# Weighted context sums of a Perceiver block: classical products against seven Strassen products, one core of a Trainium2 chip

## The chip, the core and the metric

The kernel runs on one core of one Trainium2 chip. The time is device time in microseconds for one launch, the median of three runs. A core has a matrix engine (TensorE, "PE" in the profile, with its weight loads as "PEld"), a vector engine (VectorE, "DVE"), a scalar engine (ScalarE, "ACT"), GpSimd ("POOL") and SyncE ("SP"), which here only issues transfers. Each engine works through its own queue in order; semaphores tie the queues together. All the arithmetic of this kernel is in 32-bit floats.

## The reference

One block of a Perceiver: cross attention from 8 x 64 latents to a context of 8 x 1601 rows, then causal self attention, then a feed-forward part with ternary weights, each with a residual. The change lies in the cross attention, whose core is:

```python
q = (hidden_states @ Wq).reshape(B, Sq, H, D)          # B=8, Sq=64, H=16, D=128
k = (encoder_hidden_states @ Wk).reshape(B, Skv, H, D) # Skv=1601, context width 256
v = (encoder_hidden_states @ Wv).reshape(B, Skv, H, D)
q = rmsnorm(q, gq)
k = rmsnorm(k, gk)
scores = jnp.einsum('bqhd,bkhd->bhqk', q, k) * scale
attn = jax.nn.softmax(scores, axis=-1)
out = jnp.einsum('bhqk,bkhd->bqhd', attn, v)
return out.reshape(B, Sq, H * D) @ Wo
```

The kernel never forms the values of all 1601 rows. It sums the context rows themselves with the softmax's probabilities (a 256 x 512 result for a batch and half of the heads) and multiplies by Wv afterwards. These sums are the "weighted context sums".

## The kernel before, in words

**Units and steps.** The work of cross attention is cut into 16 units `u`: a batch entry `b` and a half `g` of the heads (8 heads of 64 queries, 512 columns). A unit has 1601 context rows: 12 full blocks of 128 and a tail of 65, numbered `j` = 0 to 12. Two full blocks make a pair, and `step(u, q)` (L928) handles one pair `q` = 0 to 5. So there are 96 steps, and in the main loop the order on TensorE, VectorE, ScalarE and GpSimd is the order in which the code calls the instructions (`manual_schedule`). SyncE's transfers are placed by the framework around this.

**Keys and scores of a step.** A step needs the norms of the keys of its 256 rows (products of 128x512, called `p_u`, `p_5`, `p_2`) and the raw scores of the rows (products of 128x256, called `s_a`, `s_2`). Both are already made by Strassen's scheme in Winograd's form: seven products in place of eight, with sums of operands made on GpSimd (`cxS`, L212 to L215, from the transposed context `cxT`; `aT`, L247 to L250, from the queries) and sums of results on ScalarE and VectorE. A product in 32-bit floats is two TensorE instructions in the profile. The bank `p_u` carries a chain of growing sums: first product, copied away by ScalarE (`p1`), then a second product on top, copied (`u2`), a third on top, added to `p5` by VectorE (`c22`, L1017), and a fourth on top, whose squares ScalarE sums in place (`squares`, L720). `c12` (L999) and `c11` (L1046) are the other two blocks of keys; all four blocks are squared and summed by ScalarE in 16 pieces. At the start of the next step the squares become factors (`rsqrt_into`), VectorE scales the scores (L690) and keeps a running maximum `mx` (L704, L706).

**Softmax of the unit before.** While unit `u` grows its scores, unit `u-1` gets its probabilities: VectorE subtracts the maximum (`less_max`, L785) and ScalarE takes exponentials in place (L789) in steps 1 to 4, in portions listed in `PROBS`; GpSimd adds them up into `den` (`add_to_sums`, L796, L798), three blocks in step 1, two in step 2, three in step 3 and four in step 4. A tiny copy `gate` (L1005) keeps GpSimd from starting before the running maximum of the step is done. The maximum over rows is found in step 0 (`find_max`), and spread over the partitions by products of ones with two parts of a diagonal, a rounded high part and the rest (`spread_diag`, L735, `spread_max`, L760). The sums `den` are spread and inverted in step 5.

**Weighted sums.** `weigh_context(u, j)` (L800) adds block `j` into two banks `y0`, `y1` of 128x512: for each half of the context's columns one product of 128x512, so four TensorE instructions a block. `weigh(k)` (L918) hands out the next `k` blocks of unit `u-1`, with a lag: one behind the first `p_u`, one ahead of the third product of `p_u` (`product_7`), and in step 1 two behind `product_7` in place of the latter. `finish` (L834) multiplies the two banks by the inverted sums on VectorE, in step 1. After the loop come the last blocks of unit 14, the values of the first heads, and unit 15's softmax and weighted sums, then Wo, self attention and the feed-forward part.

**Banks and buffers.** The eight banks of PSUM: tags `k` (two, for `p_u`), `s` (two, for `s_a`, `s_2` and the tail scores), `m` (two, for `p_5`, `p_2` and spreading) and `y0`, `y1`. The tag `t2` is a set of 12 buffers of 128x512 in SBUF for everything that is kept for a while; `s` has 7 buffers of 128x2x512 for the scores; `cxn` 5 buffers of one block of context.

Of the kernel before, what the change touches and what calls it, by code (L numbers as in the profile page):

```python
# [28 lines left out]
def perceiver_kernel(  # L29
# [127 lines left out]

    xs = ctx.enter_context(ExitStack())
    ctxp = xs.enter_context(tc.tile_pool(name="ctxp", bufs=1, side="right"))

    CXN = 5
    cxn, cxT = {}, {}

    def load_context(u, j):
        b, r = u // G, rows(j)
        t = ctxp.tile([P, C], F32, tag="cxn", name="cxn", bufs=CXN)
        nc.sync.dma_start(t[:r, :], cx[b, j * P : j * P + r, :])
        cxn[u, j] = t

    NB = 4 * NC
# [3 lines left out]
    def load_blocks(b, q):  # L176

        t = ctxp.tile([P, NC, 8, 32], F32, tag="cxB", name="cxB", bufs=2)
        src = cx[b, 2 * q * P : 2 * (q + 1) * P, :].rearrange(
            "(ki kj) (c ci cj) -> ci kj c ki cj", kj=32, c=NC, cj=32  # L180
        )
        for i in range(4):
            nc.sync.dma_start(t[32 * i : 32 * i + 32], src[i])
        cxB[b, q] = t
# [7 lines left out]
    def transpose_context(b, q):  # L192
# [4 lines left out]
        t = ctxp.tile([P, NC, 2 * P], F32, tag="cxT", name="cxT", bufs=6)  # L197
# [8 lines left out]
        if (b, q) == (0, 0):  # L206
            sums = ctxp.tile([P, 4, P], F32, tag="cxB", name="cxS", bufs=2)
        else:
            sums = work.tile([P, 4, P], F32, tag="og", name="cxS", bufs=HG)
        s1, s2, s3, s4 = [sums[:, i, :] for i in range(4)]  # L210
# [451 lines left out]
    def new_ksq():  # L662
        return work.tile([P, 4, HD], F32, tag="t2", name="ksq", bufs=12)

    def tail_scores(u):
        b, g = divmod(u, G)
        sp = ps.tile([P, HG, S], F32, tag="s", name="sp")
# [30 lines left out]
    def keep_max(u, j):  # L698
# [3 lines left out]
        if j == 1:  # L702
            mx[u] = work.tile([P, HG, S], F32, tag="t2", name="mx", bufs=12)
# [4 lines left out]
    def bank(name, tag="m"):  # L708
        return ps.tile([P, 4 * HD], F32, tag=tag, name=name)

    def kept(name):
        return work.tile([P, 4 * HD], F32, tag="t2", name=name, bufs=12)
# [14 lines left out]
    def load_contexts(k):  # L727

        nonlocal n_cx
        while n_cx < min(k, NU * NJ):  # L730
            u, j = divmod(n_cx, NJ)
            load_context(u, j)
            n_cx += 1

    def spread_diag(col):  # L735
# [4 lines left out]
        lo = small.tile([P, W // P], FR, tag="clo", name="clo", bufs=2)  # L740
        nc.vector.tensor_tensor(lo, col, hi.bitcast(F32), ALU.subtract)
        dg = []
        for part in (hi, lo):
            d = work.tile([P, W // P, P], FR, tag="t2", name="dg", bufs=12)
            nc.vector.tensor_tensor(
                d,
                ident.unsqueeze(1).to_broadcast([P, W // P, P]),
                part.bitcast(F32).unsqueeze(2).to_broadcast([P, W // P, P]),
                ALU.mult,
            )  # L750
            dg.append(d.rearrange("p a k -> p (a k)"))
        return dg
# [7 lines left out]
    def spread_max(u):  # L760
        bp = spread(mB[u])
        mB[u] = work.tile([P, HG, S], F32, tag="t2", name="mB", bufs=12)
# [28 lines left out]
    def add_to_sums(u, j, eng):  # L791
        r = rows(j)
        s = s_sb[u, j]
        if j == 1:
            den[u] = work.tile([P, HG, S], F32, tag="t2", name="den", bufs=12)
# [3 lines left out]

    def weigh_context(u, j):  # L800
        b, g = divmod(u, G)
        r = rows(j)
        if j == 0:
            yps[u] = [
                ps.tile([P, HG, S], F32, tag=f"y{c}", name=f"y{c}", bufs=1)
                for c in range(NC)
            ]
        s = s_sb.pop((u, j))
        s_pair.pop((u, j // 2), None)
        for c in range(NC):  # L810
            nc.tensor.matmul(  # L811
                yps[u][c],
                cxn[u, j][:r, ts(c, P)],
                s[:r],
# [3 lines left out]

    def find_sum(u):
        rB[u] = [  # L820
            work.tile([P, W], FR, tag="t2", name=f"den{n_}", bufs=12) for n_ in "hl"
# [3 lines left out]
    def spread_sum(u):  # L825
        bp = spread(rB[u])
        rB[u] = work.tile([P, HG, S], F32, tag="t2", name="rB", bufs=12)
# [6 lines left out]
    def finish(u):  # L834

        b, g = divmod(u, G)
        for c in range(NC):
            nc.vector.tensor_tensor(
                a_sb[g][c][:, :, ts(b, S)], yps[u][c], rB[u], ALU.mult
            )  # L840

    LAG = 3
    NQ = 3 * NF
    tiles = [(b, j) for b in range(B) for j in range(NJ)]
    pairs = [(b, q) for b in range(B) for q in range(NJF // 2)]
    n_tp, n_q, n_cx, n_av = 1, 0, 0, -LAG
# [18 lines left out]
    def piece(name, single, dtype=F32):  # L865
# [772 lines left out]
```

## Time and profile before

| | |
|---|---|
| runs (us) | 1682.91, 1682.92, 1683.78; median 1682.92 |
| span of the profiled execution | 1681.5 us |
| what lies around the span, against the median | 1.4 us |
| PE busy | 1670.3 us, 99% of the span |
| DVE, ACT, POOL busy | 1193.6 (71%), 1155.3 (69%), 449.8 us (27%) |
| granted TensorE clock | 1.00 in all windows of the loop |
| one unit in the loop (start of VectorE's `chi` to the next unit's, 596.29 to 675.90) | 79.61 us |

The page's groups give for each line the summed busy time, the mean length of one instruction, and the idle time just before them with what ended it. TensorE's instructions are pipelined and their ends are modelled: a 128x512 instruction is listed with 592 ns, but the next one starts 430 ns after it. Where the cost of a product is wanted, the distance between starts has to be taken. In this document "step 1" always means `q` = 1 of a unit.

### The profile page before, as it was taken

To read this page: it belongs to the slowest core of one execution; us is meant where nothing else is said; L and a number is where in the kernel's file an instruction comes from. 1 tells how busy PE (TensorE), PEld (TensorE's weight loads), DVE (VectorE), ACT (ScalarE), POOL (GpSimd) and SP (SyncE) were. 2 spreads that over 40 slices of the span, in tenths; PEclk is the share of its full clock that TensorE was granted. 3 is DMA by queue.
4 is the path that set the end of the run, shared out by engine and by line. 5 is a ranking of instruction groups with operands and counts; after the bars stand their busy time and mean duration, and the time that the engine had idled before them with its cause. 6 is when DMAs were issued, how large, how long until landed. Compare 5 with 4: busy or idle time off the path is not lost.

```text
span 1681.5 us, 20165 instructions
## 1 busy us (share of the span) xinstructions
PE 1670.3 (99%) x5484; PEld 955.9 (57%) x5484; DVE 1193.6 (71%) x1922; ACT 1155.3 (69%) x4511; POOL 449.8 (27%) x592
## 2 busy tenths in 40 slices
PE   9999999999999999999999999999999999999999
PEld 5755555555555555555555555555555554466787
DVE  5447878787887878787878787888778786235641
ACT  5668887878787777777787878787877773023441
POOL 3312132423242323232232324232323122000040
PEclk9999999999999999999999999999999999999999
DMA  7002221212222222122222212221221216400330
GB/s 216 1 7 36 38 48 41 59 39 46 44 50 44 43 50 46 44 43 49 48 45 46 48 40 50 49 51 38 46 47 35 68 43 240 137 1 1 101 101 25
DMA packets 255769, 92.61 MB, mean 55 GB/s; under 512 B 209936, under 2 KB 236328, under 8 KB 255656
## 3 DMA queue, kind: packets, MB, share of 16 engines
q1 hardware_dynamic: 246298, 68.78, 18.6%
q0 software_dynamic: 8928, 22.02, 4.4%
q8 instruction: 43, 0.70, 0.2%
q14 instruction: 70, 0.57, 0.1%
q10 hardware_dynamic: 430, 0.53, 0.1%
HBM read 77.62 MB, written 7.34 MB: 51 GB/s over the span
## 4 chain that ended last, share of the span: by engine, by line
PE 96%; ACT 2%; DVE 2%; issue 0%; POOL 0%; POOLq 0%; DVEq 0%; ACTq 0%
PE y L811 21%; PE p_u L716 19%; PE s_a L716 14%; PE p L716 14%; PE gu L1453 4%; PE op L897 3%; PE s L716 2%; PE kp L286 2%; PE fop L1567 2%; PE mm_qk L1248 2%; PE q_u L406 2%; PE aps L502 2%; PE vp L882 2%; PE sp L669 2%; PE q L406 1%; PE bp L110 1%
## 5 line engine op out<-in xcount | busy, mean ns | idle before, releaser
L720 ACT ACTIVATE c<-c 128x128 f32<-128x128 f32 x1152 | 340.6, 297 | 140.6 <-DVE c L1017 57.7
L811 PE MATMUL y<-s,cxn 128*128 128x512 f32 x768 | 356.9, 592 | 0.0
L811 PEld LDWEIGHTS y<-s,cxn 128*128 128x128 f32 x768 | 144.5, 190 | 151.7 <-issue 138.9
L720 ACT ACTIVATION_READ_ACCUMULATOR c<-c 128x1 f32 x1152 | 215.2, 187 | 0.0
L798 POOL TENSOR_TENSOR den<-den,s 128x512 f32<-128x512 f32 x150 | 190.7, 1271 | 43.5 <-ACT s L789 36.4
L716 PEld LDWEIGHTS s_a<-aT,cxS 128*128 128x128 f32 x576 | 109.3, 190 | 137.9 <-issue 126.3
L1005 POOL COPY gate<-mx 128x1 f32<-128x1 f32 x60 | 11.0, 183 | 618.9 <-DVE mx L704 287.5
L716 PE MATMUL s_a<-aT,cxS 128*128 128x256 f32 x576 | 171.3, 379 | 0.0
L690 DVE TENSOR_TENSOR s<-s,ssq 128x1024 f32<-128x1024 f32 x96 | 116.9, 1218 | 24.9 <-ACT ssq L105 24.7
L706 DVE TENSOR_TENSOR mx<-mx,s 128x512 f32<-128x512 f32 x160 | 114.1, 713 | 7.6
L789 ACT ACTIVATE s<-s,zero_t 128x1024 f32<-128x1024 f32 (+1 forms) x117 | 115.9, 991 | 4.6 <-DVE s L785 4.6
L785 DVE TENSOR_TENSOR s<-s,mB 128x1024 f32<-128x1024 f32 (+1 forms) x117 | 116.4, 1017 | 2.2 <-ACT mB L763 2.1
L1017 DVE TENSOR_TENSOR c<-p_u,p 128x512 f32<-128x512 f32 x96 | 64.9, 676 | 71.5 <-PE p_u L716 71.5
L1042 DVE TENSOR_TENSOR s<-s_a,half 128x512 f32<-128x512 f32 x96 | 66.1, 688 | 57.1 <-POOL den L798 41.1
L720 ACT ACTIVATE p_u<-p_u 128x128 f32<-128x128 f32 x384 | 99.9, 260 | 9.3
L716 PE MATMUL p_u<-wkS,cxT 128*128 128x512 f32 x192 | 98.5, 594 | 0.9 <-DVE c L1017 0.9
L716 PE MATMUL p_u<-wkS,cxS 128*128 128x512 f32 x192 | 98.2, 593 | 0.9 <-ACT p L953 0.9
L716 PE MATMUL p<-wk,cxS 128*128 128x512 f32 x192 | 98.2, 593 | 0.0
L716 PE MATMUL p<-wkS,cxS 128*128 128x512 f32 x192 | 98.1, 592 | 0.0
L716 PE MATMUL p_u<-wk,cxS 128*128 128x512 f32 x192 | 98.0, 592 | 0.0
L716 PE MATMUL p<-wk,cxT 128*128 128x512 f32 x192 | 98.0, 592 | 0.0
L716 PE MATMUL p_u<-wk,cxT 128*128 128x512 f32 x192 | 98.0, 592 | 0.0
(239 smaller groups left out, 3254.0 us busy)
## 6 DMA issues: line engine op xcount, KB each, us to landing
cxn<-in_ctx_dram SPq DMA_DIRECT2D x192, 128.0 KB
cxB<-in_ctx_dram SPq DMA_DIRECT2D x192, 64.0 KB
wf<-in_L_ffn_w_gate_up_dram SPq DMA_DIRECT2D x32, 256.0 KB
fgu<-fw POOLq DMA_DIRECT2D x4, 2048.0 KB, 8.4
fw<-wT SPq DMA_DIRECT2D x192, 32.0 KB
wq<-in_L_xattn_Wq_dram SPq DMA_DIRECT2D x4, 1024.0 KB
wf<-in_L_ffn_w_proj_dram SPq DMA_DIRECT2D x16, 256.0 KB
wo<-in_L_xattn_Wo_dram POOLq DMA_DIRECT2D x16, 256.0 KB, 6.8
```

The source lines that it names most:

```text
L406: nc.tensor.matmul(out_, a[:, c], b[:, c], start=first, stop=True, skip_group_check=not first)
L690: nc.vector.tensor_tensor(flat, flat, kr.unsqueeze(2).to_broadcast([P, 2 * HG, S]), ALU.mult)
L706: nc.vector.tensor_tensor(mx[u][:r], mx[u][:r], s[:r], ALU.max)
L716: nc.tensor.matmul(out_, a, w, start=start, stop=True, skip_group_check=not start)
L720: nc.scalar.activation(k[:, ts(h, HD)], k[:, ts(h, HD)], AF.Square, accum_out=ssq[:, 4 * half + h : 4 * half + h + 1],)
L785: nc.vector.tensor_tensor(t, t, m.to_broadcast([r, len(js), W]), ALU.subtract)
L789: nc.scalar.activation(t, t, AF.Exp, bias=zero_t[: t.shape[0]], scale=1.0)
L798: eng.tensor_tensor(den[u][:r], den[u][:r], s[:r], ALU.add)
L811: nc.tensor.matmul(yps[u][c], cxn[u, j][:r, ts(c, P)], s[:r], start=(j == 0), stop=(j == NJ - 1),)
L1017: nc.vector.tensor_tensor(c22, p_u, p5, ALU.add)
L1042: nc.vector.tensor_tensor(quarters[:, 1::2], s_a, half[:, 0:2], ALU.add)
L1453: nc.tensor.matmul(gu[:, cols], fgu_sb[rr // 8][:, rr % 8, c, :], xs_[n_][c][:, cols], start=(c == 0 and n_ == 0), stop=(c == ND - 1 and n ...
```

## The change

The weighted sums of units 0 to 14 are made from seven products a pair of blocks instead of eight half-size ones: the 256x256 piece of context (a pair of row blocks, two halves of columns) and the 256x512 piece of probabilities are cut into 2x2 blocks, and Winograd's seven products of 128x256 go into seven half banks of four banks `y0` to `y3`. As the sums of results are linear, they are made once a unit.

- `context_sums` makes three sums of 128x128 and overwrites one block, four GpSimd operations a pair; `prob_sums` makes three sums of 128x256 (`yT`, one buffer) and overwrites a block of the probabilities, four GpSimd operations a pair.
- `pair_products` yields the seven products: three at the end of a step, two behind the next step's first `p_u`, two ahead of its `product_7`. `tail_products` adds the tail's rows in step 0.
- `gather_first` and `gather` put the seven sums together in step 1 of the unit after next: a copy on ScalarE, one 128x512 and four 128x256 additions on VectorE, two 128x256 additions on GpSimd, and the two 128x512 multiplications by the inverted sums on GpSimd; `finish` on VectorE remains for unit 15.
- Banks: `k` and `s` have one bank each, `y0` to `y3` one each, `m` two; `s_2` and the tail scores move to `m`. The squares of `c11` are moved behind those of `p_u` and the copy of the last score block.
- The maximum is rounded to its high part: `spread_diag` makes one diagonal, and the spreading product has one part.
- Context is loaded a pair at a time, three buffers of 256 rows. `t2` has 10 buffers, the scores 8; `cxS` has three sums and takes the fourth in place; other buffers move to suit. After the loop, tiles that alternated in `k` and `s` alternate with `y2` and `y3`.

The core of the diff:

```diff
-    CXN = 5
+    CXN = 3
...
+    T2 = 10
...
-        s1, s2, s3, s4 = [sums[:, i, :] for i in range(4)]
+        s1, s2, s4 = [sums[:, i, :] for i in range(3)]
+        s3 = a21
...
     def bank(name, tag="m"):
-        return ps.tile([P, 4 * HD], F32, tag=tag, name=name)
+        return ps.tile([P, 4 * HD], F32, tag=tag, name=name, bufs=2 if tag == "m" else 1)
...
-        lo = small.tile([P, W // P], FR, tag="clo", name="clo", bufs=2)
-        nc.vector.tensor_tensor(lo, col, hi.bitcast(F32), ALU.subtract)
-        dg = []
-        for part in (hi, lo):
...
+        return [d.rearrange("p a k -> p (a k)")]
...
+    def context_sums(u, p):
...
+        eng = nc.gpsimd
+        eng.tensor_tensor(s1, a21, a22, ALU.add)
+        eng.tensor_tensor(s2, s1, a11, ALU.subtract)
+        eng.tensor_tensor(s4, a12, s2, ALU.subtract)
+        eng.tensor_tensor(a21, a11, a21, ALU.subtract)
+        yA[u, p] = a11, a12, a22, s1, s2, a21, s4
...
+    def prob_sums(u, p):
+
+        (b11, b12), (b21, b22) = prob_blocks(u, p)
+        t1, t2_, n4 = [yT[:, i, :] for i in range(3)]
+        eng = nc.gpsimd
+        eng.tensor_tensor(t1, b12, b11, ALU.subtract)
+        eng.tensor_tensor(t2_, b22, t1, ALU.subtract)
+        eng.tensor_tensor(b12, b22, b12, ALU.subtract)
+        eng.tensor_tensor(n4, b21, t2_, ALU.subtract)
+
+    def pair_products(u, p):
...
+        for k, h, a, b_, first in (
+            (0, 0, a11, b11, True),
+            (1, 0, a12, b21, True),
+            (2, 0, s4, b22, True),
+            (0, 1, s1, t1, False),
+            (1, 1, s2, t2_, False),
+            (3, 1, s3, t3, True),
+            (2, 1, a22, n4, False),
+        ):
+            product(yps[u][k][:, ts(h, W // 2)], a, b_, first and p == 0)
+            yield
...
+    def gather_first(u):
+
+        y0, y1 = yps[u][:2]
+        c15 = kept("c15")
+        nc.scalar.copy(c15, y0)
+        cu = kept("cu")
+        nc.vector.tensor_tensor(
...
+        cw = kept("cw")
+        nc.gpsimd.tensor_tensor(
+            cw[:, : W // 2], cu[:, W // 2 :], c15[:, W // 2 :], ALU.add
+        )
...
+    def gather(u):
...
+        add = nc.vector.tensor_tensor
+        add(u3, q7, u2, ALU.add)
+        c21 = c15[:, : W // 2]
+        add(c21, q4, u3, ALU.add)
+        add(u3, t22, u3, ALU.add)
+        add(u2, q3, u4, ALU.add)
+        nc.gpsimd.tensor_tensor(c5, u3, c5, ALU.add)
+        b, g = divmod(u, G)
+        for c, t in enumerate((cu, c15)):
+            nc.gpsimd.tensor_tensor(
+                a_sb[g][c][:, :, ts(b, S)],
+                t.rearrange("p (h s) -> p h s", s=S),
+                rB[u],
+                ALU.mult,
+            )
...
+    def pair_of(u, q):
+        v, p = (u - 1, q - 1) if q else (u - 2, NQU - 1)
+        return (v, p) if v >= 0 else None
...
     def step(u, q):
...
-        if u > 0:
-            weigh(1)
-        elif q < n_tails - 1:
+        weigh(2)
+        if q == 1 and u > 1:
+            gather_first(u - 2)
+        if new:
+            context_sums(*new)
+        if u == 0 and q < n_tails - 1:
...
+        weigh(9)
+        if q == 0 and u > 1:
+            tail_products(u - 2)
+        if q == 1 and u > 1:
+            gather(u - 2)
         if probs:

             nc.gpsimd.tensor_copy(gate, mx[u][:, 0, 0:1])
         for js in probs:
             for j in js:
                 add_to_sums(u - 1, j, nc.gpsimd)
...
+        if new:
+            prob_sums(*new)
+        if u > 1 or (u == 1 and q > 1):
+            load_contexts(n_cx + (2 if q == 0 else 1))
...
         product_7()
         squares(ssq[:, 1], 1, c22)
-        if u > 0 and q == 1:
-            weigh(2)
...
-        squares(ssq[:, 0], 0, c11)
         next(roots, None)
         product(p_u, a22, n4, False)
         squares(ssq[:, 1], 0, p_u)
-        s_2 = ps.tile([P, 4, S], F32, tag="s", name="s_2")
+        s_2 = bank("s_2")[:, : 4 * S].rearrange("p (h s) -> p h s", s=S)
...
         nc.scalar.copy(quarters[:, 2], s_a[:, 1])
+        squares(ssq[:, 0], 0, c11)
+        if new:
+            under_way = pair_products(*new)
+            weigh(3)
...
-        for jw in range(NJ - LAG, NJ):
-            load_contexts((last - 1) * NJ + jw + CXN)
-            weigh_context(last - 1, jw)
+        context_sums(last - 1, NQU - 1)
+        weigh(9)
+        prob_sums(last - 1, NQU - 1)
         find_max(last)
+        tail_products(last - 1)
         mB[last] = spread_diag(mB[last])
-        finish(last - 1)
+        under_way = pair_products(last - 1, NQU - 1)
+        weigh(5)
+        gather_first(last - 1)
+        weigh(9)
+        load_contexts(NU * NY)
+        gather(last - 1)
```

## The prediction

> **What bounds the kernel now.** The page comes first: who is busy, what chain ended last, and the costliest groups.
>
> ```profile
> PE 1670.3 (99%) x5484; PEld 955.9 (57%) x5484; DVE 1193.6 (71%) x1922; ACT 1155.3 (69%) x4511; POOL 449.8 (27%) x592
> ...
> PE 96%; ACT 2%; DVE 2%; issue 0%; POOL 0%; POOLq 0%; DVEq 0%; ACTq 0%
> ...
> L811 PE MATMUL y<-s,cxn 128*128 128x512 f32 x768 | 356.9, 592 | 0.0
> ```
>
> TensorE never stops: every microsecond of products that goes is won, and every wait that comes is paid. Second, the waits of TensorE; each kind comes to under 3 us, so the other engines have some cover everywhere, but the view does not say how much.
>
> ```profile
> PE p_u L716 <- ACT p L953: 0.9, 2, 0.7
> PE p_u L716 <- DVE c L1017: 0.9, 2, 0.4
> ```
>
> Third, the timeline of TensorE for the true price of a product (two instructions a line, distance between starts).
>
> ```profile
> 592.35 0.59 PE L716 MATMUL s_a<-a,cxT 128*128 128x256 f32 x2
> 592.78 1.02 PE L716 MATMUL p_u<-wkS,cxS 128*128 128x512 f32 x2
> 593.64 1.02 PE L716 MATMUL p<-wk,cxS 128*128 128x512 f32 x2
> ```
>
> A 128x256 product costs 0.43 us, a 128x512 one 0.86: half the columns, half the time, weight load hidden. Fourth, step 1 of a unit, where the change puts most of its new work: the stretch that begins with its first `p_u`, then the timelines of VectorE, TensorE and GpSimd in it, then two groups of GpSimd by form.
>
> ```profile
> 601.85:616.89 15.04, 15.04 (x44) 7.97 (x43) 11.56 (x19) 11.34 (x47) 5.75 (x8) 1.00 0.21 44
> ```
>
> ```profile
> 605.00 1.28 DVE L838 TENSOR_TENSOR a<-y,rB 128x512 f32<-128x512 f32 x2
> ...
> 610.41 0.65 DVE L1017 TENSOR_TENSOR c<-p_u,p 128x512 f32<-128x512 f32 x1
> ```
>
> ```profile
> 609.15 3.60 PE L811 MATMUL y<-s,cxn 128*128 128x512 f32 x8
> ...
> 614.31 1.02 PE L716 MATMUL p_u<-wkS,cxT 128*128 128x512 f32 x2
> ```
>
> ```profile
> 612.37 2.62 POOL L798 TENSOR_TENSOR den<-den,s 128x512 f32<-128x512 f32 x2 [1.62 <-ACT s L789]
> ```
>
> ```profile
> L247 POOL TENSOR_TENSOR aT<-a 128x256 f32<-128x256 f32 x16 | 14.2, 888 | 65.9 <-issue 34.4 <-PE s_a L716 31.5
> ...
> L249 POOL TENSOR_TENSOR aT<-a,a 128x256 f32<-128x256 f32 x16 | 11.9, 743 | 13.7 <-PE s_a L716 13.7
> ```
>
> VectorE ends `c22` (L1017) only 3.2 us ahead of the `p_u` product that needs it, and the two blocks of `weigh(2)`, 3.44 us, are what stands between. GpSimd is busy 5.8 of 15 us; its sums of 512 columns follow each other every 1.31 us (two in 2.62; the mean of one in the groups is 1.27).
>
> **What is won.** A pair of blocks now takes four products of 512, 3.44 us; after, seven of 256, 3.01 us. The tail costs 1.72 us both ways. Six pairs in 15 units: 90 x 0.43 = 38.7 us. The spreading of the maximum loses its second part, an instruction of 0.22 us, in 16 units: 3.5 us. Together 42.2 us off TensorE, all on the path.
>
> [...] The rows above show 215 and 430 ns here, and they are used.
>
> **What is added on GpSimd.** A pair: four sums of 128x128 at 0.46 (the `cxS` groups' mean) and four of 128x256 at about 0.77 (743 to 888 in the rows), 4.9 us; a unit's `gather`: two of 128x256 at 0.73 (L250's mean) and two multiplications of 512 columns at 1.31 (the nearest row is `den`), 4.1 us. A unit's 24.5 us of GpSimd become about 58 of 80. On the whole it fits; in step 1 it does not. There the code sets GpSimd's order: the small `cw`, `context_sums`, `gather`'s sum and two multiplications, `gate`, three `den` sums, and only then `prob_sums`, whose first two results TensorE wants as its second and third product of step 2. Clock from step 1's first `p_u`:
>
> - TensorE ends the last two products of the old pair at 6.45: four key products 3.44, three of `s_a` 1.29, four of y 1.72.
> - VectorE starts late, since the bookkeeping of step 0's weights (L622 to L633, 2.4 us) now ends at 1.0; then `less_max` 1.14, `cu` behind ScalarE's copy `c15` (2.6 to 3.3), `less_max` to 4.4, scaling to 5.7, maximum to 6.3, `c12` to 6.9. The additions depend on each other, 0.45 us each: the third is done at 8.2.
> - GpSimd: 8.3 + 0.73 + 2 x 1.31 + 0.15 (`gate`) + 3 x 1.31 = 15.7; first result of `prob_sums` 16.5, second 17.25.
> - TensorE, unhindered, starts step 2 at 12.04 (seven products each of 0.86, 0.43 and 0.43) and wants these two at 12.90 and 13.33. The second can start at about 17.35.
>
> So 4.0 us are lost from step 1 to step 2. About 0.8 of that falls in step 1: VectorE does the fourth addition, a transpose and `c22` until 9.8, and the fourth `p_u` product, wanted at 9.03, waits, as `weigh(2)` no longer stands ahead of it. The rest is the wait for `prob_sums`. It is one loss, not two. Bounds: with no gap between instructions (1.27, 0.73) and VectorE never late, 3.3; with all GpSimd work stretched as L247 is against L249 (888 to 743), 5.8. I take 4.0, since the chain is made of rows of the same shapes. Units 2 to 15: 14 x 4.0 = 56 us. Later steps catch up: in step 2 GpSimd has two `den` sums, and its second result comes 1 us ahead of need. In step 4, with four, it is about 0.6 us ahead; if that is gone, 0.5 us a unit.
>
> **One bank for growing keys.** The next step's first `p_u` now waits for the squares of the last.
>
> ```profile
> 1370.22 0.25 ACT L720 ACTIVATE p_u<-p_u 128x128 f32<-128x128 f32 x1
> ...
> 1370.62 0.26 ACT L720 ACTIVATE p_u<-p_u 128x128 f32<-128x128 f32 x1
> ```
>
> Each piece starts 0.40 after the one before, so the four take 1.6 us, and where ScalarE is free they start 0.25 after the product: 1.85. Between stand `s_2`, the last `s_a` and three products of y: 2.15. It fits by 0.3 where ScalarE is on time. In step 4 it is not: there its queue has three exponentials, and the old cover of 1.72 us ahead of `product_7` is 0.86; the squares end some 0.4 too late. I take 0.3, bounds 0 and 0.6, in 15 units: 4.5 us. In unit 0 and step 0 of unit 1 there are no y products: 0.86 of cover for 1.85, seven times 1.0; TensorE's waits in that stretch (2.7 us) are partly taken up: 6 us, bounds 3 and 10.
>
> **After the loop** the values wait for `gather` of unit 14: 1.35 of additions, 0.73 and 2.62 on GpSimd, where `finish` took 1.28: 4 us, bounds 2 and 6.
>
> **Costed at nothing.** VectorE: `finish`, `clo` and a diagonal go (2.1 us a unit), 2.3 come; what matters is counted above. ScalarE: one copy more. SyncE's loads: as many bytes, issued behind the y products that free the buffer, a step and a half ahead of use; if late, `context_sums` waits, which has some 2 us of cover in step 1. Ten `t2` buffers: `p1` and `p5` of step 2 wait for `gather`'s multiplications, done at 10.4 and 11.7, ahead of both. `c11` of step 1 waits for GpSimd's sum at 9.0, earlier than its own product.
>
> **The sum**, against the execution's own time (span 1681.5 plus 1.4, the median 1682.9): 1682.9 - 42.2 + 56 + 4.5 + 6 + 4 = 1711.2; I say 1711.
>
> **Rivals.** *A, the other side: GpSimd keeps up.* If the products of step 2 found `prob_sums` ready, because the wait is short or TensorE has other delays in front that cover it, the sum is 1682.9 - 42.2 + 14.5 = 1655. It decides at a wait of (42.2 - 14.5) / 14 = 2.0 us a unit: below that the change is faster. For it: GpSimd idles 73% of the time, and no TensorE wait on it is seen now. Against: the chain is queue order, and half of it is five operations of a length the profile shows 150 times.
>
> *B: the doubled work on GpSimd and VectorE slows both.* Stretched by a fifth, the chain is 1.8 us longer: 14 x 1.8 = 25 us more, 1736. For: 888 against 743 ns for one shape. Against: `den` keeps 1.27 beside a busy VectorE. [...]
>
> *C: single banks cost a wait in every step.* If ScalarE is late by 0.4 us beyond the margin in half of the 90 steps, 18 us more, 1729; in all, 1747. For: ScalarE is at 62 of 80 us a unit and would have 77. Against: squares of `c11` are moved out of the way.
>
> **How the numbers follow.** Forecast 0.55, A 0.1, B 0.15, C 0.15; the rest, 0.05, is a wait somewhere near 2 us, on either side of the old time. Forecast's own bounds: 3.3 us gives 1701, the others' lower ends 1692; upper ends with 4.6 us 1728. The range runs from 1692 to 1738, which takes in B and half of C and leaves A out. A measurement of this kernel can tell about 0.2%, 3.4 us. Faster 0.11, same 0.02, slower 0.87.
>
> **What would show it.** Right: a TensorE wait on GpSimd's L853 or L854 of about 3 us, 14 times, one on VectorE's `c22` of some 0.8 in step 1, a unit of 81 us, and the span of y instructions cut by 38 us. Wrong: no such wait (A), GpSimd's 512-column sums over 1.4 us (B), or first `p_u` products that wait on ScalarE in most steps (C).

## The result

The changed kernel takes 1890.04 us (median of four runs, 1888.44 to 1893.08) against 1683.08 for the kernel before on the same chip: a ratio of 1.1232, 95% interval 1.1218 to 1.1246. It is 12% slower. The forecast was 1711 with a range up to 1738; the sign was right and the size was not.

The profiled execution has a span of 1888.9 us, 207.4 more than before. First the lines of its page that answer to those shown of before (busy time, the chain that ended last, the costliest group of the weighted sums with the idle time ahead of it):

```profile
PE 1723.1 (91%) x6068; PEld 1079.5 (57%) x6068; DVE 1376.1 (73%) x1935; ACT 1163.4 (62%) x4526; POOL 1165.4 (62%) x1372
...
PE 57%; DVE 18%; POOL 14%; ACT 7%; issue 3%; DMA 0%; POOLq 0%; DVEq 0%; ACTq 0%
...
L732 PE MATMUL y<-yT,yS 128*128 128x256 f32 x360 | 115.2, 435 | 66.5 <-POOL yT L853 48.3
```

TensorE was hardly ever idle before (11.2 us of the span) and is idle for 165.8 us now. The chain, which was 96% TensorE, runs through VectorE and GpSimd for a third of the time. Two things in the first line are odd. VectorE has 13 instructions more and is busy for 182 us more. And TensorE is busy for 53 us more, although 42 us of products were taken away.

The waits of TensorE, longest in total first (us in total, times, longest):

```profile
PE y L732 <- POOL yT L853: 48.3, 21, 5.2
PE bp L110 <- DVE st L694: 27.5, 12, 3.0
PE p_u L732 <- ACT p_u L736: 20.3, 16, 1.7
PE y L732 <- POOL yT L854: 18.1, 24, 1.2
```

The first and the last are the wait for `prob_sums`: of the 21 waits for L853, 14 stand in step 2, where the prediction has them, and 7 of 1.0 to 1.3 us in step 5 of every second unit. The second is in no step of it: the spreading product of step 5 waits for a bank `m` that the tail scores hold until VectorE has read them (L694).

Where it happens is seen in windows of one unit, cut at each step's first `p_u` (columns: window, length, busy time of TensorE, its weight loads, VectorE, ScalarE, GpSimd, then the granted clock). The steps 0 to 5 of this unit last 14.67, 13.27, 18.81, 12.05, 14.59 and 20.46 us; the same unit before had 13.37, 14.18, 12.46, 12.47, 12.46 and 14.67. These are steps 2, 3 and 5:

```profile
681.53:700.34 18.81, 15.56 (x44) 9.40 (x43) 12.80 (x16) 10.46 (x45) 17.81 (x22) 0.82 0.20 39
700.34:712.39 12.05, 12.05 (x44) 7.98 (x43) 11.13 (x16) 9.93 (x43) 8.39 (x10) 1.00 0.21 44
...
726.98:747.44 20.46, 16.68 (x49) 9.27 (x48) 16.43 (x23) 9.70 (x44) 16.30 (x22) 0.92 0.08 11
```

Step 3 has no wait and is the change as it was meant: 12.47 became 12.05, 0.42 less. Steps 2 and 5 lose 6.4 and 5.8 us, and in both the granted clock is below 1. The timeline of TensorE and one more window show the second half of that price:

```profile
685.17 1.22 PE L732 MATMUL y<-yT,yS 128*128 128x256 f32 x2 [2.62 <-POOL yT L853]
687.02 1.22 PE L732 MATMUL y<-yT,yS 128*128 128x256 f32 x2 [0.63 <-POOL yT L854]
688.04 1.91 PE L732 MATMUL p<-wkS,cxS 128*128 128x512 f32 x2
```

```profile
685.17:692.00 6.83, 6.20 (x11) 3.69 (x12) 5.00 (x5) 0.89 (x2) 6.65 (x7) 0.50 0.25 29
```

The `p` product at 688.04 is followed by the next one 1.70 us later, not 0.86. From the end of the 2.62 us wait TensorE runs at half its clock for 6.83 us. Over the whole span the mean granted clock is 0.968; as it is either 1.00 or 0.50 (in all 552 whole windows of the grid below), 6.4% of the span, 121 us, ran at half, and that costs 60 us of full-speed products. This is most of why TensorE is "busy" for longer with less to do: 53 us more, and 42 us of products less, make 95. The other 35 are what a wait costs beyond its idle time. In step 1 the product ahead of the wait for `c22` starts at 676.43, the one behind it at 678.40 and the next at 679.37, which is 1.22 us more than twice 0.86, for a wait listed with 0.95. At 0.27 us each, the some 120 waits that came would make 32 us (an estimate). So the loss adds up: 155 us of idle time, 60 of halved clock and 35 of this, less 42 of products, are 208.

A wait of 2.62 us was enough for this. All the changes of the clock in this trace lie a whole number of 3.413 us apart (the halvings at 685.17 and 736.37, for example, 15 of them). Four windows of this grid follow: one with the wait of 2.62 us, one with most of a wait of 2.97 (for L694, until 736.78), and two that share another wait for L694 of 2.96 (until 922.42):

```profile
681.76:685.17 3.41, 0.79 (x3) 0.01 (x1) 3.34 (x3) 1.91 (x9) 3.27 (x3) 1.00 0.03 4
...
732.96:736.37 3.41, 0.86 (x4) 0.40 (x3) 3.34 (x4) 1.17 (x2) 3.23 (x4) 1.00 0.00 0
...
917.28:920.69 3.41, 2.00 (x7) 1.06 (x6) 3.38 (x4) 1.17 (x2) 3.25 (x5) 1.00 0.00 0
920.69:924.11 3.42, 1.69 (x5) 1.05 (x6) 2.31 (x4) 0.67 (x2) 3.22 (x5) 1.00 0.00 0
```

TensorE is busy for 0.79 and 0.86 us in the first two, and the clock is halved from the end of each, before the 0.63 us wait in the one case and inside the wait in the other. It is busy for 2.00 and 1.69 us in the last two, and the clock stays. In the kernel after, a window at full clock with 1.93 us of idle time or more was always followed by half clock (26 windows), one with 1.67 us or less never, and of nine in between one. So a wait's place on the grid counts as well as its length.

Last, what VectorE and GpSimd do to each other. Both timelines in step 1, VectorE first:

```profile
671.16 1.22 DVE L795 TENSOR_TENSOR s<-s,mB 128x1024 f32<-128x1024 f32 x1
672.29 1.75 DVE L706 TENSOR_TENSOR s<-s,ssq 128x1024 f32<-128x1024 f32 x1
```

```profile
671.32 1.64 POOL L905 TENSOR_TENSOR cw<-cu,c 128x256 f32<-128x256 f32 x1 [9.07 <-DVE cu L898]
672.92 1.44 POOL L838 TENSOR_TENSOR yS<-cxn 128x128 f32<-128x128 f32 x1
```

They take turns. GpSimd's `cw` (0.73 us alone) is issued at 671.32, but VectorE's `less_max` is running, to 672.38; `cw` ends 0.58 later, at 672.96. VectorE's scaling (1.22 alone) is issued at 672.29 and ends at 674.04, 1.08 after `cw`. GpSimd's `L838` (0.46 alone) ends at 674.36, 0.32 after the scaling. What is left to each behind the other (0.58, 1.08 and 0.32) is its length alone less 0.14 or 0.15. So neither looks slowed while it works: all but that of an instruction comes after the other's end.

### The profile page after: what moved, and what is told of

Read it like the earlier page. It is cut to its first block, busy times and chain, and to the rows that moved or that the text cites. A ratio compares the mean times of both kernels' runs of the same rounds, so it can differ in the third digit from the quotient of the medians.

```text
span 1888.9 us, 22249 instructions
## 1 busy us (share of the span) xinstructions
PE 1723.1 (91%) x6068; PEld 1079.5 (57%) x6068; DVE 1376.1 (73%) x1935; ACT 1163.4 (62%) x4526; POOL 1165.4 (62%) x1372
## 4 chain that ended last, share of the span: by engine, by line
PE 57%; DVE 18%; POOL 14%; ACT 7%; issue 3%; DMA 0%; POOLq 0%; DVEq 0%; ACTq 0%
PE p_u L732 10%; PE p L732 8%; PE y L732 8%; PE s_a L732 7%; POOL den L808 5%; PE gu L1593 3%; DVE s L706 3%; PE op L1019 3%; DVE s L795 2%; ACT c L736 2%; DVE mx L722 2%; POOL yT L854 2%; ACT p_u L736 2%; PE fop L1711 2%; PE mm_qk L1388 2%
## 5 line engine op out<-in xcount | busy, mean ns | idle before, releaser
L732 PE MATMUL p_u<-wk,cxT 128*128 128x512 f32 x384 | 198.8, 599 | 20.6 <-ACT p_u L736 20.3
L808 POOL TENSOR_TENSOR den<-den,s 128x512 f32<-128x512 f32 x150 | 193.4, 1290 | 13.8 <-ACT s L799 5.6
L732 PE MATMUL y<-yT,yS 128*128 128x256 f32 x360 | 115.2, 435 | 66.5 <-POOL yT L853 48.3
L1107 ACT COPY p<-p 128x512 f32<-128x512 f32 x96 | 56.0, 583 | 170.1 <-PE p L732 170.1
L732 PE MATMUL y<-s,cxn 128*128 128x256 f32 x540 | 147.2, 382 | 0.0
L732 PEld LDWEIGHTS y<-yT,yS 128*128 128x128 f32 x360 | 69.2, 207 | 133.8 <-POOL yT L853 70.7
L1126 DVE TENSOR_TENSOR c<-p,u 128x512 f32<-128x512 f32 x96 | 65.6, 683 | 83.9 <-PE p L732 83.9
L732 PE MATMUL s_a<-aT,cxS 128*128 128x256 f32 x384 | 119.9, 395 | 0.0
L732 PE MATMUL p_u<-wkS,cxT 128*128 128x512 f32 x192 | 101.7, 611 | 15.8 <-DVE c L1138 15.6
L732 PE MATMUL s_a<-aT,cxT 128*128 128x256 f32 x384 | 114.3, 379 | 0.0
L856 POOL TENSOR_TENSOR yT<-s,yT 128x256 f32<-128x256 f32 x90 | 83.9, 932 | 46.7 <-PE y L732 46.7
L732 PEld LDWEIGHTS y<-s,cxn 128*128 128x128 f32 x540 | 102.4, 192 | 13.8
```

The lines of the kernel that those rows point to most:

```text
L732: nc.tensor.matmul(out_, a, w, start=start, stop=True, skip_group_check=not start)
L808: eng.tensor_tensor(den[u][:r], den[u][:r], s[:r], ALU.add)
L856: eng.tensor_tensor(n4, b21, t2_, ALU.subtract)
L1107: nc.scalar.copy(p5, p_5)
L1126: nc.vector.tensor_tensor(c12, p_5, u2, ALU.add)
```

## The experiments

Four theories were told apart. **Shared access**: a GpSimd sum and a VectorE instruction with two inputs in SBUF exclude each other, as the lines above suggest. **Queue**: the loss is the order in GpSimd's queue in step 1, as predicted. **Banks**: single banks, and the tail scores in `m`. **Clock**: each long wait is paid a second time in halved clock. Ratios are against the kernel before, with 95% intervals.

### The sums without anyone who waits for them

`b_dummy` is the kernel before with idle sums on GpSimd (product with itself of a scratch tile `dq`); `b_memset` has memsets in their place.

```diff
+        if q == 1 and u > 1:
+            extra(256, 1)
+        if has_pair(u, q):
+            extra(128, 4)
         if u > 0:
             weigh(1)
...
                 add_to_sums(u - 1, j, nc.gpsimd)
+        if has_pair(u, q):
+            extra(256, 4)
```

> The kernel before, with the added GpSimd work as idle work: per pair four products of 128x128 and four of 128x256 on a scratch tile of their own, per unit six more of 128x256, at the places of the new sums in GpSimd's queue. No instruction waits for their results. Theory 'shared access' (a GpSimd sum and a VectorE instruction with two inputs in SBUF exclude each other): VectorE's mx goes from 713 to over 830 ns, its bf16 multiplications from 425 to 502 to over 800 ns, GpSimd's 128x128 sums from 455 to over 600 ns, and VectorE gains over 100 us of busy time; the time rises by 20 to 120 us since the kernel before has some cover for a late VectorE. Theory 'queue' (the loss is GpSimd's order in step 1, as predicted): all these durations stay within 5% and the time within 10 us of 1683.

Measured: 1733.43 us, 1.0299 (1.0284 to 1.0315), 50 us more. Two groups of VectorE, the running maximum and one multiplication in bf16, the format in which VectorE prepares the ternary weights (before: 713 and 502 ns):

```profile
L706 DVE TENSOR_TENSOR mx<-mx,s 128x512 f32<-128x512 f32 x160 | 125.5, 785 | 7.6
...
L640 DVE TENSOR_TENSOR m<-m,sg 128x512 bf16<-128x512 bf16 x48 | 38.0, 793 | 0.0
```

VectorE gains 100 us of busy time (1193.6 to 1293.3) with the same instructions. The maximum rose less than expected (785, not 830), and so did the bf16 multiplications (to 590, 674 and 793, not over 800). The rest came out as shared access says, the idle 128x128 sums with 669 ns among it; of the durations named, none stayed within the 5% of the queue theory.

> As the run before it, but the idle work is memsets of 128x256, which write and read nothing: one for a 128x128 sum, two for a 128x256. Theory 'shared access' through reads: VectorE's mx stays below 740 ns and the time within 5 us of 1683, although GpSimd is busy for longer. If writing is enough to exclude VectorE: mx over 800 ns again and a time near that of the other idle kernel. Theory 'queue': both idle kernels at 1683.

Measured: 1692.66 us, 1.0057 (1.0042 to 1.0072). The same two groups:

```profile
L706 DVE TENSOR_TENSOR mx<-mx,s 128x512 f32<-128x512 f32 x160 | 115.9, 724 | 7.6
...
L640 DVE TENSOR_TENSOR m<-m,sg 128x512 bf16<-128x512 bf16 x48 | 22.4, 467 | 0.0
```

GpSimd is busy for 900.9 us, twice as long as before, and VectorE hardly notices. The 10 us that remain, 5 more than expected, are mostly a wait for `cxS` (6.1 us), whose own sums were pushed back in the queue. So it is the reading that excludes: in the kernel before it costs 41 us (1733.4 against 1692.7), though nothing waits for the idle sums.

### The sums taken out, and replaced

`a_nosums` is the kernel after without the eight sums a pair.

```diff
-        eng.tensor_tensor(s1, a21, a22, ALU.add)
...
-        yA[u, p] = a11, a12, a22, s1, s2, a21, s4
+        yA[u, p] = a11, a12, a22, a21, a22, a21, a12
...
-        t1, t2_, n4 = [yT[:, i, :] for i in range(3)]
+        t1, t2_, n4 = t3, b22, b21
```

> The kernel after without context_sums and prob_sums: the seven products take raw blocks in their place, so the weighted sums are not the reference's. All else stays: seven products a pair, banks, gather. Theory 'shared access' or 'queue': the waits on L853, L854 and most of those on the tail scores go, the granted clock is back at 1.00; 1683 - 42 + 15 to 30 for gather and banks = 1655 to 1670. Theory 'banks' (single banks for keys and scores, tail scores in m): more than half of the loss stays, over 1780.

Measured: 1738.99 us, 1.0331 (1.0316 to 1.0347). Between the theories: 151 us of the loss go with the sums, and 56 over the old time stay, where all but banks had expected a gain. Its two longest waits:

```profile
PE p_u L732 <- ACT p_u L736: 27.2, 36, 1.4
PE bp L110 <- DVE st L694: 20.6, 15, 1.9
```

`a_memset` puts memsets of the same tiles in the same places of the queue, with the same products waiting for them.

```diff
+        for t in (t1, t2_, b12, n4):
+            for _ in range(2):
+                eng.memset(t, 1.0)
```

> The kernel after with each of the eight sums a pair made for the products replaced by two memsets of the same result tile (some 0.4 us for 128x128 and 0.6 us for 128x256), in the same places of GpSimd's queue and with the same instructions waiting for them; the weighted sums are not the reference's. GpSimd is busy nearly as long but reads nothing in them. Theory 'shared access': VectorE's mx returns from 871 to below 740 ns, its bf16 multiplications from 927 to 1068 to 600 to 850 as in the kernel without these sums, and the time is 1739 (that kernel) to 1770. Theory 'queue': products still wait for L853's successor after the den sums in step 1, some 3 us in 14 units, the clock still halves behind them, and the time stays over 1820.

Measured: 1780.23 us, 1.0579 (1.0563 to 1.0594), clock 0.988. First the wait for the sums, then the maximum's group:

```profile
PE y L732 <- POOL yT L854: 35.1, 14, 4.2
```

```profile
L722 DVE TENSOR_TENSOR mx<-mx,s 128x512 f32<-128x512 f32 x160 | 114.9, 718 | 8.6
```

The time lies between the two bands, and both theories hold for a part. The wait of the prediction is there though the eight sums exclude nobody, 14 times 2.5 us on average: queue and its clock cost 41 us (1780.2 against 1739.0). The other 110 us (1890.0 against 1780.2) come only where the sums read. The memsets for the 128x256 sums are some 0.1 us shorter than the sums, which may move a few us from the one to the other. That the sums need operands and the memsets none does not count: in the kernel after the sums wait for no operand, only for products that still read the buffers they overwrite (52 us ahead of L853 and L856).

`a_noctx` leaves out `context_sums` alone.

> The kernel after without context_sums (four 128x128 sums a pair; the products take raw blocks of context), prob_sums left on GpSimd. All eight sums cost 151 us. If what counts is the time in which GpSimd reads, the four small ones are 1.6 of 4.4 us: 56 us less, 1834. If what counts is the number of instructions that VectorE can collide with, they are half: 75 us less, 1815. If only prob_sums matter, because TensorE waits for them: over 1870.

Measured: 1897.67 us, 1.1272 (1.1255 to 1.1289): 8 us slower than with them. The time lies where only `prob_sums` would matter, but that does not show that the small sums exclude for nothing: the wait of `bp`, 27.5 us in the kernel after, has grown by more than the other waits shrank. In unit 6, without the four small sums `prob_sums` of step 5 starts sooner, against VectorE's scaling (1.74 us for 1.22) and maximum, and the tail scores behind these come as late as before, while TensorE is there earlier:

```profile
PE bp L110 <- DVE st L694: 63.1, 15, 4.8
```

`a_dve` moves the eight sums to VectorE (`eng = nc.vector`, with the order of `a_order` below).

> The kernel after with the eight sums a pair on VectorE in place of GpSimd (and GpSimd's order as in a_order, so that the first den sum comes ahead of prob_sums). Theory 'shared access': a sum takes half as long on VectorE and excludes nobody for long; GpSimd is busy some 560 us and its other sums return to their old lengths; but VectorE gets 96 x 8 sums more, 1.6 us for four of 128x256 and 1.0 for four of 128x128, 15 us a unit on 64, so it becomes late itself: 1760 to 1840. Theory 'queue': VectorE is now the queue that is late, as long as GpSimd was: 1860 or more.

Measured: 2010.14 us, 1.1947 (1.1926 to 1.1968), clock 0.945. Shared access had it too fast by 170 us; the 1860 or more of the queue theory takes it in. GpSimd's other sums are back at 473 to 512 ns and the maximum at 710, as shared access says, but VectorE is now the late one:

```profile
PE p_u L732 <- DVE c L1138: 210.0, 75, 4.3
```

### The order in the queues

`a_order` puts `prob_sums` ahead of the `den` sums and of `gather` on GpSimd.

```diff
+        if q == 1 and u > 0:
+            nc.gpsimd.tensor_copy(gate, mx[u][:, 0, 0:1])
+            for j in js[:2]:
+                add_to_sums(u - 1, j, nc.gpsimd)
+            js = js[2:]
+        if new:
+            prob_sums(*new)
         if q == 1 and u > 1:
             gather(u - 2)
...
-        if new:
-            prob_sums(*new)
```

> The kernel after with another order in GpSimd's queue: in step 1 the sum den of the first two blocks, then prob_sums, then gather's GpSimd operations, then the other den sums; in steps 2 to 4 prob_sums ahead of the den sums. Nothing else changes. Theory 'queue': the wait on L853 (48.3 us) and the halved clock behind it go, some 1815. Theory 'shared access': the work on both engines stays as long as it is; the waits on L853 shrink by less than 25 us or turn up at other places, the time stays over 1850.

Measured: 1879.69 us, 1.1169 (1.1150 to 1.1187), 10 us less. The waits for `yT` are gone entirely, and others have taken their place:

```profile
PE bp L110 <- DVE st L694: 58.4, 15, 4.7
PE p_u L732 <- DVE c L1138: 44.4, 55, 1.2
```

`a_tail` lets VectorE do the tail scores ahead of the scaling in step 5 and the three bf16 operations behind it.

> The kernel after with VectorE's order in step 5 changed: the tail's scores (L694) come ahead of the scaling and the maximum of the last pair, and the three bf16 operations of signed behind these. Theory 'queue behind L694': the wait of bp on L694 (27.5 us) goes, and with it the halved clock behind it in the even units; 1850 to 1865. Theory 'shared access': VectorE's work in step 5 is as long as before and only the order differs; c12 or the banks p_5 and p_2 come late in its place, the time stays over 1878.

Measured: 1886.12 us, 1.1208 (1.1193 to 1.1223), 4 us less. The wait on L694 is gone; `c22` waits 37.3 us instead of 15.6, with up to 3.4 at once. VectorE in step 5 is late in this order too.

`a_tail3` moves the tail scores to step 3 (`if q == 3: tail_scores(u)`), and `a_order_tail3` makes both changes of order.

> The kernel after with the tail scores (two products, L694 and its maximum) moved from step 5 to step 3 of a unit, so that no spreading product stands behind them in the banks m. Theory 'banks': the wait of bp (27.5 us) and the halved clock behind it in the even units go and nothing of the size takes their place, 1845 to 1865. Theory 'shared access and VectorE late in step 5': c22 or c12 are late in its place, as when VectorE's order was changed: 1880 or more.

Measured: 1874.13 us, 1.1140 (1.1121 to 1.1158), 16 us less, between the two bands. The wait of `bp` on L694 is gone, but `cxS` is waited for twice as long (L228: 15.3 us for 7.7) and more of the span ran at half clock (0.958).

> Both changes of order together: prob_sums ahead of the den sums and gather on GpSimd, and the tail scores in step 3. Each alone left waits of the other kind. If the two losses add up: 1880 - 58 (wait of bp in a_order) - clock 25 = near 1800. If they are the same work on VectorE and GpSimd that turns up elsewhere: over 1850.

Measured: 1826.84 us, 1.0855 (1.0838 to 1.0871), clock 0.993. The time is between the two expectations. The two together bring 63 us where each alone brought 10 and 16; it looks as if one long wait a unit, as long as it is left, takes in what the other lets go. Of the waits, what is left is mostly VectorE's and ScalarE's lateness in small portions:

```profile
PE p_u L732 <- DVE c L1138: 57.9, 60, 1.9
PE p_u L732 <- ACT p_u L736: 41.4, 38, 1.7
```

`a_memset_ot` has both orders and the memsets of `a_memset`: the change as it would be if its eight sums a pair excluded nobody.

> The kernel with memsets in place of the eight sums, with both changes of order (prob_sums ahead of the den sums and gather; tail scores in step 3): what the change would take if its sums excluded nobody and their place in the queues were better. Theory 'queue 41 us, shared access 110, banks the rest': no wait for yT, none of bp on L694: 1780 - 41 - 30 = 1700 to 1715, so that even then it would be slower than the kernel before. If a time under 1683 comes out, banks and gather cost less than the runs so far say.

Measured: 1728.86 us, 1.0267 (1.0249 to 1.0284). 14 us above the expected band, and still 45 us slower than before: the rest of the change does not pay either.

### The banks

`b_bank` is the kernel before with one bank each for `p_u` and `s_a`, and with `s_2` and the tail scores in `m`; one block of the weighted sums moves to the end of the step.

```diff
-        s_2 = ps.tile([P, 4, S], F32, tag="s", name="s_2")
+        s_2 = bank("s_2")[:, : 4 * S].rearrange("p (h s) -> p h s", s=S)
...
-        squares(ssq[:, 0], 0, c11)
...
         nc.scalar.copy(quarters[:, 2], s_a[:, 1])
+        squares(ssq[:, 0], 0, c11)
+        if (u > 0 or q == NQU - 1) and (u, q) != (last, NQU - 1):
+            weigh(1)
```

> The kernel before with the banks of the kernel after: one bank for p_u, one for s_a, s_2 and the tail scores in m, the squares of c11 behind those of p_u; one block of y stands at the end of each step in place of behind the next first p_u, so that the cover for the squares is 2.58 us (2.15 in the kernel after). Products, GpSimd and gather as before. Theory 'banks' (what is left of the loss without the sums, some 95 us, is waits for single banks): waits of p_u on its squares and of bp on L694 as in the kernel after, 1715 to 1750. Theory 'gather and order': below 1695.

Measured: 1734.01 us, 1.0305 (1.0289 to 1.0321). The banks alone take 51 us, and the longest wait, 30.1 us, is for the tail scores; `p_u` waits for its squares only 7 times, 5.8 us in all:

```profile
PE bp L110 <- DVE st L678: 30.1, 15, 2.6
```

`a_nosums_tail3` is `a_nosums` with the tail scores in step 3.

> The kernel without the eight sums a pair (the products take raw blocks) and with the tail scores in step 3. Theory 'banks': the wait of bp on L694 there (20.6 us with some 7 us of halved clock and drained pipelines) goes, 1703 to 1715; what is left over 1641 is single banks for p_u, gather and the end. Rival 'VectorE late in step 5 whatever the order': 1730 or more.

Measured: 1717.31 us, 1.0199 (1.0184 to 1.0214), just above the band. So 22 us are the tail scores in `m`. Over 1641 stay 77 us. Of these 51 are waits: `p_u` on its own squares, with those of unit 0 (27.2 us, 36 times), `c22` (16.7), and at the end the values (4.1) and the last maximum (2.8); halved clock (0.997) is some 5. The rest is not placed. As `p_u` waited for only 5.8 us in `b_bank`, with 0.43 us more of cover, the one bank is not the whole cause of the 27.2; what `gather` adds was not run by itself.

### The clock, and the rounded maximum

`a_fill` repeats a product of step 2 so that TensorE works where it would wait.

```diff
-        product(p_u, a11, b11, True)
+        for _ in range(4 if u > 1 and q == 2 else 1):
+            product(p_u, a11, b11, True)
```

> The kernel after with the first p_u product of step 2 made four times over in the units 2 to 15 (the same result each time), so that TensorE works for 2.58 us where it waits 2.63 us for L853: 36 us of useless products. Theory 'clock follows idle time': the halved stretches of step 2 (3.4 or 6.8 us in each of 14 units, 65 us, worth 32 us of products) disappear, the mean granted clock rises from 0.968 to about 0.985 and the time falls by 20 to 35 us, to 1855 to 1870, with more work done. Theory 'clock has another cause': the clock stays near 0.968 and the time at 1890 or, as p1 and the squares come later, up to 1920.

Measured: 1883.61 us, 1.1194 (1.1179 to 1.1209): 36 us of useless products more, and 6 us less in time. Span and mean clock:

```profile
core 0: 1881.8 us, clock 0.985
```

No halved stretch is left in step 2 of units 2 to 14 (unit 15, which waited for 5.2 us, keeps one of 3.41), and the clock's share of the loss goes from 60 to 28 us. That the clock follows TensorE's idle time is shown by this and by the windows above. The expected 20 to 35 us did not arrive, because `bp` (32.2 us, 14 times), `c22` (22.4) and `cxS` (19.0) wait for longer; some of it I can't place.

`b_round` is the kernel before with one diagonal in `spread_diag` and one part in the spreading product.

> The kernel before with the rounded maximum alone: one spreading product of 0.22 us less in 16 units and two VectorE operations less. All theories: 3.5 us less, 1679.4; if VectorE's shorter queue in step 0 saves nothing more. Over 1682 would say that the second product is hidden.

Measured: 1679.03 us, 0.9977 (0.9967 to 0.9986), 3.8 us less. It is faster than both kernels, and the only part of the change that was seen to pay.

## Why the prediction was right and wrong

The runs make a chain from the products' gain to the measured time:

| from | to | us | what lies between |
|---|---|---|---|
| 1682.9 | 1640.7 | -42 | products, worked out |
| 1640.7 | 1717.3 | +77 | single banks for `p_u` and `s_a`, `gather`, unit 0, the end, not told apart (`a_nosums_tail3`) |
| 1717.3 | 1739.0 | +22 | tail scores in `m` (`a_nosums`) |
| 1739.0 | 1780.2 | +41 | place in GpSimd's queue (`a_memset`) |
| 1780.2 | 1890.0 | +110 | exclusion of VectorE and GpSimd (kernel after) |

The steps are not independent, as the runs on the order show; another way through them would share the sum out differently. Nor is the 77 free of exclusion: without the eight sums VectorE's bf16 multiplications still take 745 to 851 ns (425 to 502 before), beside GpSimd's other sums.

**What is won, 42.2 us: right.** Step 3 is 0.42 shorter, where 0.43 a pair was worked out, and `b_round` is 3.8 faster where 3.5 was. A product of 256 columns costs half of one of 512 in the kernel after as well, 0.43 and 0.86 us between starts.

**14 x 4.0 us in step 1: right in place, near in size as a wait, and short as a loss.** TensorE waits for L853 and L854 in units 2 to 14 together 3.3 to 3.8 us, where 3.2 was worked out, and for `c22` 0.95 where 0.8 was. That it is so near is in part luck: in unit 6 the second result comes 18.7 us after step 1's first `p_u`, not 17.25, because its sum takes 1.78 us and not 0.77, while TensorE comes late itself. As time, steps 1 and 2 of unit 6 take 32.1 us, where 12.04 + 12.04 + 4.0 = 28.1 was forecast; the difference is mostly halved clock. Where the eight sums exclude nobody, the queue costs 41 us against the 56 of the sum. Both waits that the prediction gave as its signs are in the trace, and yet the unit is not 81 but 92 to 94 us long.

**The step that failed is the price of a sum, "0.46" and "0.77", with nothing put down for VectorE ("what matters is counted above"), and with it rival B's "a fifth longer, 1736".** In the kernel after a sum of 128x128 takes 0.70 us on average and one of 128x256 0.97, a unit's GpSimd work is 72 us and not 58, and VectorE is busy for 182 us more. What the reading sums add is 110 us of the 207 (`a_memset`), where B had 25. That the two engines slow each other was named there, and priced from 888 against 743 ns. Two misreadings led there. One was "`den` keeps 1.27 beside a busy VectorE". In the rows below it keeps it, and the price is paid on VectorE. So the sign given for B, sums of 512 columns over 1.4 us, did not come either: `den` took 1290 ns on average, 19 more than before. In the kernel after, step 5, this is a VectorE operation on 128x8 elements, 0.17 us alone, and below it GpSimd's sum at that time:

```profile
726.51 0.68 DVE L640 TENSOR_SCALAR scl<-tot 128x8 bf16<-128x8 f32 x1
...
735.96 0.68 DVE L694 TENSOR_TENSOR st<-sp,krP 65x512 f32<-65x512 f32 x1
```

```profile
725.89 1.27 POOL L808 TENSOR_TENSOR den<-den,st 65x512 f32<-65x512 f32 x1
```

The tiny operation ends at 727.19, with the end of `den` at 727.16. With several of these in front of L694, `bp` waits 2.97 us for it (2.2 at most in `a_memset`). The other misreading was that rows were taken as their means: the 888 ns of L247 is the mean of 16 sums that took from 726 to 1673. The kernel before shows the exclusion, in the column of minimum, median and maximum of one line:

```profile
L624 DVE TENSOR_SCALAR scl<-tot x48: 170/171/718, 135.8 to 1370.7; 128x8 bf16<-128x8 f32 x48
```

An operation of 171 ns that sometimes takes 718 has met something, and this one runs beside `cxS` (at 654.24, for example, it takes 0.71 beside L213 and L214). With its one operand it took 250 ns on average before and takes 349 after; the maximum, with two operands in SBUF, took 718 and 724 ns beside memsets and 785 to 907 beside sums. `c22`, with one of its two operands in a bank, took no longer (676 ns before, 671 beside idle sums, 668 after; at 603.73 there, beside `den`, 0.69 us), nor did the reciprocals, with one operand in SBUF (909, 907 and 910); what sets these apart was not shown. Taken with the turns in step 1, where all but 0.14 or 0.15 us of an instruction came after the other's end, this says that the new GpSimd time fell due on one or the other engine wherever VectorE had an instruction like the first two at hand, and a fifth is not its measure.

**One bank, "4.5" and "6": the first mis-sized, the second right.** Unit 0 loses 6.2 us. In the other units `p_u` waits for its squares in 8 places, all in step 5, where the prediction looked for it, but for 1.73 us each: 13.9 us, not 4.5. And the tail scores in `m`, moved there by the change, were not looked at for who waits behind them; `bp` does, 27.5 us, and the sum has no term for it. `b_bank` puts all the banks at 51 us.

**After the loop, "4 us, bounds 2 and 6": right for the wait it prices, short for the stretch.** `gather`'s multiplications keep the values waiting for 4.2 us. But from the last step's first `p_u` to the end some 20 us more go by than before: the last maximum keeps TensorE waiting for 3.9 us, the last `bp` for 2.6, and three halvings of the clock cost 6.8.

**What no step had: the clock.** 60 us of the loss are products at half clock behind waits, and some 35 what each wait costs beyond its idle time. The prediction counts a wait as its idle time alone; with 155 us of idle time more and 42 of products less, even a right sum of waits would be short by 95 of the 207.

**Rival C** was right in kind and not in size: the first `p_u` waits on ScalarE in 16 steps of 96, not in most. Of the 20.3 us, 6.4 are unit 0 and the steps next to it; the 13.9 of the others are 9.4 over the 4.5 of the sum, where C had 18 more. Rival A fell.

**Two sums of the prediction are off by a little.** Its terms for the stretch after the loop, 1.35 + 0.73 + 2.62 - 1.28, make 3.4 and not 4. The upper ends with 4.6 us make 1730 and not 1728, and the 4.6 is not worked out. Neither bears on the result.

## What to carry to other kernels

Sums that read SBUF, added here on GpSimd, were paid for by VectorE too, instruction by instruction (the running maximum, with two operands in SBUF, went from 713 to 871 ns); look for such a price in the maximum of short VectorE operations (718 ns where the median was 171), not in means, and count what stands behind these ahead of a product. With TensorE at 99%, price a wait at itself plus some 0.3 us (the estimate of 0.27 above), and where waits take some 2 us out of 3.4, add 1.7 to 3.4 us, what the 3.41 or 6.83 us at half clock cost here. When a tile changes its bank, list who asks for that bank next.

## What the runs showed of the hardware that was not expected

- TensorE's clock halved behind a single wait of 2.62 us, for 6.83 us in one place and for 3.41 in others; a wait of 2.97 us for L694 was followed by it in 4 of 7 units. It went with the idle time in one window of the 3.413 us grid: in the kernel after, 1.93 us or more were always followed by half clock, 1.67 us or less never. Useless products in place of the wait kept the clock up (`a_fill`, 0.985 for 0.968).
- GpSimd's memsets of 128x256 took 311 ns each, and 1236 of them beside VectorE's two-input operations left VectorE's running maximum at 724 ns (713 before); sums on the same engine, which read, raised it to 785 (idle sums) and 871 (kernel after).
- Four of the eight sums a pair less made the kernel 8 us slower (`a_noctx`): the waits they left came back at another place, larger.
